# The place of n's own-column matmuls in the order of TensorE, in a convolution layer followed by a scan of GRU columns

## The chip, the cores and the metric

The kernel runs on one core of a Trainium2 chip. The metric is the device time of one execution in microseconds (us). A core has five engines that each work through their own queue: TensorE (PE, matmuls; its weight loads are shown apart as PEld), VectorE (DVE), ScalarE (ACT), GpSimd (POOL) and SyncE (SP, which issues transfers here). They meet through semaphores.

## The reference

The input x is 4 images of 64 channels by 256 by 256, in fp32. Layer 0 normalizes it by groups, runs a 1x1 and a depthwise 3x3 convolution, multiplies 8x8 patches in the frequency domain, normalizes and gates the product, projects it back and adds it to x. Layer 1 normalizes the sum by groups and then goes through it column by column. Each column depends on the one before it:

```python
def step(prev_col, cur_col):
    nb = jnp.concatenate([pad, prev_col, pad], axis=1)
    x = jnp.concatenate([nb[:, :-2], nb[:, 1:-1], nb[:, 2:]], axis=-1)
    new = _gru_cell(x.reshape(B * H, 3 * Cf), cur_col.reshape(B * H, Cf), ...)
# _gru_cell(x, h): i_r, i_z, i_n = x @ w_ih.T + b_ih;  h_r, h_z, h_n = h @ w_hh.T + b_hh
r = jax.nn.sigmoid(i_r + h_r)
z = jax.nn.sigmoid(i_z + h_z)
n = jnp.tanh(i_n + r * h_n)
return (1.0 - z) * n + z * h
```

So a row of the new column needs three neighbouring rows of the previous new column (the "taps") and one row of its own normalized input (the "own" part). The first column passes through unchanged; the other 255 are computed. The result is added to the layer's input.

## The kernel before, in words

Layer 0 works in 32 blocks and keeps TensorE busy with small fp32 matmuls. Its sums are written to a DRAM tensor `x1`. The change does not touch it.

Layer 1 starts with loads of the columns from `x1` (`load_columns`), eight columns to a buffer, and normalizes them eight columns ahead (`normalize`, on ScalarE, result `xn`). The two halves of the partitions hold the channels of different images, and `xt` is a copy of `xn` with the halves exchanged, brought by transfers on SyncE's queue, two columns at a time. The loop over `w` calls `column(w)` and then `add(w)`, in which GpSimd adds the new column to its input and, every second column, SyncE's queue stores two columns to the output.

`column(w)` lays down the matmuls. A column of 256 rows is cut in two ranges ("parts"). Part 0 of the next column is always one row shorter than the last, so that its taps need only rows of the previous column's part 0. The cut moves from 144 rows down to 113 in 32 columns, and then starts over at 144; then part 0 needs rows of both parts of the column before.

Every product with a weight is made as four matmuls on the four quarters of the array (`quarters`, 64 rows by 64 columns each), for two images a half. `own(ps, gate, h0, h1, stop)` issues the products with the column's own input: 8 matmuls in the executed program. `taps(ps, gate, h0, h1, start)` issues three neighbours: 24 matmuls. Gates go to four PSUM tiles of two banks each: `hn` (n's own part, for the whole column at once, never mixed with the taps since r multiplies it), `hr` (r: own and taps summed), `ni` (n's taps) and `hz` (z: own and taps). Each has one buffer, and the four fill the eight banks. `hr`, `ni` and `hz` are used by part 0 and then by part 1; `hn` is written once for a column and read by both parts. The trace calls them `pshn`, `pshr`, `psni` and `pshz`.

`state(w, part, ...)` turns these into the new rows. ScalarE makes g = sigmoid(hr), and then normalizes a column that will be needed eight columns later. VectorE multiplies g with `hn` (a scalar_tensor_tensor, `n<-pshn,bias_sb,g`), adds `ni`; ScalarE makes the tanh and z = sigmoid(hz); VectorE does `g<-xn,n`, `g<-g,z` and `st<-g,n`, and the last is the new state, which the next column's taps read.

All instructions of the kernel body pass through `InOrder`, which keeps each engine's queue in the order of the program's text. So what stands earlier in `column` comes earlier in TensorE's queue. A matmul that writes a PSUM tile must wait until its last readers are done: for `hn` that is the product of part 1 of the column before. Because of the recording layer, all lines of the trace read L156; tiles tell them apart.

Of the kernel before, what the change touches and what calls it, by code (L numbers as in the profile page):

```python
# [16 lines left out]
B, C, W, H = 4, 64, 256, 256  # L17
# [144 lines left out]
def tile_conv_then_gru(  # L162
# [521 lines left out]
    with ExitStack() as s:  # L684
# [60 lines left out]
        def parts(w):  # L745


            at = H // 2 + SKEW // 2 - (w - 1) % SKEW
            return (0, at), (at, H)
# [3 lines left out]
        def bank_pair(gate, w):  # L753
            return ps_g.tile([P, 2, 512], F32, tag=gate, name=f"ps{gate}_{w}")

        def quarters(ps, weights, rhs, start, stop):
            for r, c in QUARTERS:
                nc.tensor.matmul(
                    ps[c * C : (c + 1) * C, r],
                    lhsT=weights[r * C : (r + 1) * C],  # L760
                    rhs=rhs(r, c),
                    start=start,
                    stop=stop,
                    tile_position=(r * C, c * C),
                )

        def column(w):

            i, xn, xt, st = w % WB, xns[w // WB], xts[w // WB], stcols[(w - 1) // WB]

            def own(ps, gate, h0, h1, stop):

                quarters(
                    ps,
                    wh[:, gate, :],
                    lambda r, c: (xn[:, c] if r == c else xt)[r * C : (r + 1) * C, i, h0:h1],
                    True,
                    stop,
                )

            def taps(ps, gate, h0, h1, start):
                for t in range(3):
                    quarters(
                        ps,
                        wi[:, 3 * gate + t, :],
                        lambda r, c: st[r * C : (r + 1) * C, c, (w - 1) % WB, h0 + t : h1 + t],
                        start and t == 0,
                        t == 2,
                    )

            pn = bank_pair("hn", w)[:, :, 0:H]
            own(pn, 2, 0, H, True)
            for part in range(2):
                h0, h1 = parts(w)[part]
                pr, pi, pz = (bank_pair(gate, f"{w}_{part}")[:, :, 0 : h1 - h0] for gate in ("hr", "ni", "hz"))
                own(pr, 0, h0, h1, False)
                taps(pr, 0, h0, h1, False)
                taps(pi, 2, h0, h1, True)
                own(pz, 1, h0, h1, False)
                taps(pz, 1, h0, h1, False)  # L800
                state(w, part, pn[:, :, h0:h1], pr, pi, pz)

        def state(w, part, pn, pr, pi, pz):
            h0, h1 = parts(w)[part]
            i, num = w % WB, h1 - h0
            xn, st = xns[w // WB], stcols[w // WB]
            g = gk.tile([P, 2, MAX], F32, tag=f"g{part}", name=f"g_{w}_{part}")[:, :, 0:num]
            n = gk.tile([P, 2, MAX], F32, tag=f"n{part}", name=f"n_{w}_{part}")[:, :, 0:num]
            z = gk.tile([P, 2, MAX], F32, tag=f"z{part}", name=f"z_{w}_{part}")[:, :, 0:num]
            nc.scalar.activation(g, pr, AF.Sigmoid, bias=b_rz[:, 0:1], scale=1.0)  # L810
            if w + WB < W:
                normalize(w + WB, part)
            nc.vector.scalar_tensor_tensor(n, pn, bias_sb[:, 5:6], g, ALU.add, ALU.mult)
            nc.vector.tensor_tensor(n, pi, n, ALU.add)
            nc.scalar.activation(n, n, AF.Tanh, bias=bias_sb[:, 2:3], scale=1.0)
            nc.scalar.activation(z, pz, AF.Sigmoid, bias=b_rz[:, 1:2], scale=1.0)
            nc.vector.tensor_tensor(g, xn[:, :, i, h0:h1], n, ALU.subtract)
            nc.vector.tensor_tensor(g, g, z, ALU.mult)
            nc.vector.tensor_tensor(st[:, :, i, 1 + h0 : 1 + h1], g, n, ALU.add)
# [8 lines left out]
        for w in range(W):  # L828
            n, i = w // WB, w % WB
            if i == 0 and n + 1 < W // WB:  # L830
                empty_states(n + 1)
            if w:
                column(w)
            add(w)
            if i % 2 and w + 2 * WB < W:
                load_columns(w + 2 * WB - 1)
# [55 lines left out]
```

## Time and profile before

| what | value |
|---|---|
| median of 3 runs | 5957.78 us (5954.8 to 5962.69) |
| profiled execution: its own time | 5951.97 us |
| profiled execution: span, first to last instruction | 5950.2 us |
| mean granted TensorE clock | 0.994 |
| TensorE matmul busy | 5537.8 us (93%) |
| VectorE busy | 4085.5 us (69%) |
| ScalarE busy | 3465.8 us (58%) |
| GpSimd busy | 399.5 us (7%) |
| layer 1: first matmul of n to the end | 4383.2 to 5950.2 us |

The span is the time from the first to the last instruction of the profiled execution; its own time also holds what lies around these. Busy time of TensorE is modelled from pipelined matmuls, so a share of 93% doesn't say that no more matmuls would fit. A line of the order in time gives the start, the length, the engine, the operation, the tiles as out<-in with their shapes, how many instructions are merged, and in brackets the idle time of the engine before it and what ended this. A wait for several semaphores is put down to the one that came last.

### The profile page before, as it was taken

Reading aid. Unit: us, or ns where it says so; the run is one execution under the profiler, and the core shown is the slowest. Engines: PE = TensorE matmul, PEld = TensorE weight load, DVE = VectorE, ACT = ScalarE, POOL = GpSimd, SP = SyncE. Lnnn points to the kernel's source line nnn. Section 1 sums busy time; section 2 is a strip of 40 time slices with the busy share of each in tenths; the row PEclk is TensorE's granted clock in tenths of the full one; section 3 lists DMA queues with packets and bytes.
Section 4 is the critical chain, followed back from the end, with each engine's and each line's share of the span. In section 5 each row is a group of like instructions: output and inputs, shape, how many; then the busy total and the mean of one; then the engine's idle time right before and its main releaser. Section 6 shows DMA issues by size and latency. Waiting matters only on the chain.

```text
span 5950.2 us, 278865 instructions
## 1 busy us (share of the span) xinstructions
PE 5537.8 (93%) x127184; PEld 4770.7 (80%) x127184; DVE 4085.5 (69%) x9549; ACT 3465.8 (58%) x4617; POOL 399.5 (7%) x602
## 2 busy tenths in 40 slices
PE   5499999999999999999999999999979999999998
PEld 4478888888887888887888888888868888888887
DVE  7566776676676666676666767766666766676666
ACT  1256665666665656665565666565645555555555
POOL 0000000000000000000000000000002212122121
PEclk9999999999999999999999999999989999999999
DMA  9544545445445444444444554544444444444442
GB/s 384 213 133 144 139 132 147 121 141 144 140 126 142 137 135 141 140 134 133 143 124 138 146 144 123 149 131 132 128 119 113 113 113 113 113 112 113 111 113 80
DMA packets 549698, 817.79 MB, mean 137 GB/s; under 512 B 38443, under 2 KB 432436, under 8 KB 544404
## 3 DMA queue, kind: packets, MB, share of 16 engines
q1 hardware_dynamic: 523264, 683.80, 40.4%
q0 software_dynamic: 22320, 114.70, 5.8%
q8 instruction: 996, 16.32, 1.1%
q10 hardware_dynamic: 2934, 1.46, 0.1%
q14 instruction: 184, 1.51, 0.1%
HBM read 622.22 MB, written 144.05 MB: 129 GB/s over the span
## 4 chain that ended last, share of the span: by engine, by line
PE 64%; DVE 18%; ACT 7%; DMA 5%; issue 5%; SPq 0%; DVEq 0%; ACTq 0%; POOL 0%; POOLq 0%
PE psring L156 61%; DVE g L156 7%; DVE n L156 6%; DVE st L156 4%; ACT n L156 4%; DMA t<-t_all 2%; DMA xc<-in_x 2%; ACT v L156 2%; ACT z L156 1%; PE pshr L156 1%; PE pshz L156 1%; PE psni L156 1%; ACT h L156 1%; PE pshn L156 0%; SPq L156 0%
## 5 line engine op out<-in xcount | busy, mean ns | idle before, releaser
L156 PEld LDWEIGHTS psring<-h,t 100*32 100x32 f32 x40960 | 1336.1, 116 | 266.6 <-issue 184.8
L156 PE MATMUL psring<-h,t 100*32 100x128 f32 x40960 | 1437.4, 274 | 88.8 <-ACT h L156 35.6
L156 PEld LDWEIGHTS psring<-w_sb,xq 64*100 64x100 f32 x24576 | 1352.4, 163 | 86.1 <-issue 48.8
L156 PE MATMUL psring<-w_sb,xq 64*100 64x128 f32 x24576 | 1394.2, 271 | 27.3 <-POOL xq L156 17.8
L156 ACT COPY h<-psring 100x1024 f32<-100x1024 f32 x1274 | 1203.2, 1027 | 147.7 <-PE psring L156 140.9
L156 DVE TENSOR_TENSOR pr<-psring,q 128x512 f32<-128x512 f32 (+1 forms) x576 | 463.8, 860 | 338.6 <-PE psring L156 334.7
L156 DVE BATCH_NORM_STATS2 lnst<-z 128x6 f32<-128x64 f32 x4096 | 544.8, 212 | 118.7 <-ACT z L156 118.7
L156 DVE TENSOR_TENSOR z<-z,lnm 128x1024 f32<-128x1024 f32 x512 | 612.6, 1217 | 8.7
L156 ACT ACTIVATE n<-n,bias_sb 128x288 f32<-128x288 f32 (+7 forms) x510 | 259.8, 509 | 574.0 <-DVE n L156 574.0
L156 ACT COPY q<-psring 128x1024 f32<-128x1024 f32 x256 | 259.1, 1012 | 514.2 <-PE psring L156 457.6
L156 ACT COPY z<-psring 128x2048 f32<-128x2048 f32 x128 | 238.8, 1866 | 502.2 <-PE psring L156 485.1
L156 PE MATMUL psring<-pr,g_sb 32*64 32x512 f32 x8192 | 486.1, 598 | 7.2 <-issue 7.1
L156 ACT ACTIVATE y<-psring,ln_sb 128x512 f32<-128x512 f32 x512 | 372.1, 781 | 200.8 <-PE psring L156 197.2
L156 DVE COPY h<-psring 100x1024 f32<-100x1024 f32 x262 | 320.3, 1223 | 218.5 <-PE psring L156 216.2
L156 PE MATMUL pshr<-st,wi 64*64 64x144 f32 (+7 forms) x12240 | 433.3, 270 | 14.0 <-DVE st L156 13.4
L156 PE MATMUL psni<-st,wi 64*64 64x144 f32 (+7 forms) x12240 | 438.4, 270 | 8.0 <-issue 6.6
L156 DVE TENSOR_TENSOR g<-xn,n 128x288 f32<-128x288 f32 (+7 forms) x510 | 217.3, 426 | 325.2 <-ACT n L156 325.2
L156 PE MATMUL pshz<-st,wi 64*64 64x144 f32 (+7 forms) x12240 | 436.6, 269 | 1.8 <-issue 1.1
L156 DVE TENSOR_TENSOR y<-psring,y 128x1024 f32<-128x1024 f32 x256 | 312.3, 1220 | 122.7 <-ACT y L156 121.2
L156 POOL TENSOR_TENSOR raw<-raw,st 128x512 f32<-128x512 f32 x256 | 303.4, 1185 | 1208.1 <-DVE st L156 511.1
L156 PEld LDWEIGHTS pshr<-st,wi 64*64 64x64 f32 x12240 | 361.7, 133 | 17.0 <-issue 16.7
L156 PEld LDWEIGHTS psni<-st,wi 64*64 64x64 f32 x12240 | 361.5, 133 | 13.5 <-issue 9.9
(94 smaller groups left out, 6944.7 us busy)
## 6 DMA issues: line engine op xcount, KB each, us to landing
t<-t_all SPq DMA_DIRECT2D x768, 400.0 KB
xq<-in_xh POOLq DMA_DIRECT2D x128, 800.0 KB, 4.6
xc<-in_x SPq DMA_DIRECT2D x32, 2048.0 KB
xr<-in_x SPq DMA_DIRECT2D x256, 256.0 KB
x<-xr SPq DMA_DIRECT2D x256, 256.0 KB
raw<-x SPq DMA_DIRECT2D x128, 256.0 KB
raw<-x SPq DMA_DIRECT2D x256, 128.0 KB
xt<-xn SPq DMA_DIRECT2D x256, 128.0 KB
```

What stands on the lines that cost most here:

```text
L156: return self.tc.keep_in_program_order(got(*args, **kwargs))
```

## The change

In `column`, the call that issues n's own matmuls for the whole column moves from ahead of the loop over the two parts into it. In part 0 it now stands behind r's own matmuls and r's taps, and ahead of n's taps. Part 1 does not issue it, as before. The same matmuls are issued, with the same operands, into the same tiles.

```diff
             pn = bank_pair("hn", w)[:, :, 0:H]
-            own(pn, 2, 0, H, True)
             for part in range(2):
                 h0, h1 = parts(w)[part]
                 pr, pi, pz = (bank_pair(gate, f"{w}_{part}")[:, :, 0 : h1 - h0] for gate in ("hr", "ni", "hz"))
                 own(pr, 0, h0, h1, False)
                 taps(pr, 0, h0, h1, False)
+                if part == 0:
+                    own(pn, 2, 0, H, True)
                 taps(pi, 2, h0, h1, True)
                 own(pz, 1, h0, h1, False)
                 taps(pz, 1, h0, h1, False)
```

In the built program the order of VectorE, ScalarE, GpSimd and SyncE is the same as before. On TensorE each column's order becomes r of part 0, n's own part, n's taps of part 0, z of part 0, and then part 1 as before. VectorE's product of part 0 waits for TensorE and ScalarE, where it waited for ScalarE; r's taps of part 0 wait for VectorE by themselves.

## The prediction

> **What bounds the kernel now.** I read the share of each slice first, then the waits of layer 1, then the order in time of one column, then the chain of a column where the two ranges start over. The columns of layer 1 run from about 4,383 us to the end, 255 of them. In that stretch TensorE is busy 93% of the time (1394.5 of 1500 us from 4440 us on), VectorE 70%, ScalarE 58%. That looks like a TensorE bound, and the waits seem to agree (who waited | for whom: us in total, times, longest; 4650 to 5940 us):
>
> ```profile
> ACT n L156 <- DVE n L156: 482.2, 427, 2.1
> DVE g L156 <- ACT n L156: 273.0, 428, 1.0
> PEld pshn L156 <- DVE n L156: 115.1, 195, 0.9
> PE pshn L156 <- DVE n L156: 67.7, 179, 0.7
> PE pshr L156 <- DVE st L156: 11.5, 6, 1.9
> ```
>
> The third and fourth lines are what the change touches: TensorE waits for the one bank pair `hn`, which the product of part 1 of the last column (`n<-pshn`) still reads. But TensorE idles there, so it has time left; the first two lines are a loop between VectorE and ScalarE. VectorE over one column, in order of time (start, length, operation):
>
> ```profile
> 5200.53 0.40 DVE L156 TENSOR_TENSOR st<-g,n 128x230 f32<-128x230 f32 x1
> 5200.84 0.50 DVE L156 SCALAR_TENSOR_TENSOR n<-pshn,bias_sb,g 128x280 f32<-128x280 f32 x1
> 5201.45 0.45 DVE L156 TENSOR_TENSOR n<-psni,n 128x280 f32<-128x280 f32 x1
> 5202.55 0.45 DVE L156 TENSOR_TENSOR g<-xn,n 128x280 f32<-128x280 f32 x1 [0.66 <-ACT n L156]
> 5203.11 0.45 DVE L156 TENSOR_TENSOR g<-g,z 128x280 f32<-128x280 f32 x1
> 5203.60 0.45 DVE L156 TENSOR_TENSOR st<-g,n 128x280 f32<-128x280 f32 x1
> 5203.96 0.45 DVE L156 SCALAR_TENSOR_TENSOR n<-pshn,bias_sb,g 128x232 f32<-128x232 f32 x1
> ...
> 5206.47 0.40 DVE L156 TENSOR_TENSOR st<-g,n 128x232 f32<-128x232 f32 x1
> 5206.79 0.50 DVE L156 SCALAR_TENSOR_TENSOR n<-pshn,bias_sb,g 128x278 f32<-128x278 f32 x1
> ```
>
> Five instructions of part 0, five of part 1, the tanh the only idle time. The next column's product starts at 5206.79, 0.08 us before the last `st` ends (5206.47 + 0.40): back to back. From `st` to `st` it is 5.94 us. The same count over 248 columns gives a median of 5.96 us and 5.94 to 6.04 in nearly all. Does that product wait for TensorE? TensorE and ScalarE around it:
>
> ```profile
> 5204.47 0.43 PE L156 MATMUL pshn<-xn,wh 64*64 64x256 f32 x1 [0.49 <-DVE n L156]
> 5204.95 0.28 PE L156 MATMUL pshr<-xn,wh 64*64 64x139 f32 x1
> 5205.90 0.89 PE L156 MATMUL psni<-st,wi 64*64 64x139 f32 x24
> 5206.15 0.49 ACT L156 ACTIVATE g<-pshr,b_rz 128x278 f32<-128x278 f32 x1 [0.30 <-PE pshr L156]
> ```
>
> The sigmoid of r ends at 5206.64, and VectorE needs it at 5206.79. VectorE starts about 0.02 us after a ScalarE release (tanh 5201.99 + 0.53, next start 5202.55), so TensorE's order has 0.13 us to spare here. The VectorE-ScalarE loop sets the column. It isn't so in the columns where part 0 jumps from 113 to 144 rows (w = 33, 65, ... 225: seven, 7.8 us or more each) and in the first. Their chain:
>
> ```profile
> 4981.14 0.47 DVE st L156
> 4981.61 0.14 issue
> 4981.75 1.00 PE pshr L156 x24
> 4982.75 0.02 issue
> 4982.77 0.51 ACT g L156
> ```
>
> Here the taps of r need rows of part 1, so the path runs through TensorE.
>
> **What the Trainium skill says.** "PSUM — Partial Sum Buffer", section "Engine vs sequencer instructions": TensorE's matmuls start and complete in program order, so what stands behind the wait of n stands still too. The trace agrees: r's first matmul follows 0.48 us behind n's. "VectorE: DVE Perf Modes", section "Two Vector instructions with no wait between them": a wait handled by the sequencer alone doesn't make the next Vector instruction held behind the one before. The trace agrees, with numbers below. "TensorE: Matmul & The Clock Gate", section "What's actually happening": half clock until about 3.4 us of activity. In the first column r's matmuls follow each other at 0.24 us in one quarter, and a quarter later in the run takes 0.12.
>
> **The change part by part.** Nothing is added to or taken from the work: 8 matmuls with 8 weight loads (pshn) move behind 32 (pshr, part 0). No DMA moves. Times are against the profiled execution (span 5950.2, time 5951.97 us); the median of 5957.78 lies 5.8 us above that.
>
> *Ordinary columns, 246 or so.* r's own matmuls need only its bank (ScalarE freed it at 5203.24) and the column's input; its taps need `st` of part 0, at 5204.05. TensorE is done with z of part 1 at 5203.98. So r runs from about 5204.05, not 5204.95: 0.9 us earlier. n's matmuls (0.43 us when they follow other work) stand at about 5204.95 to 5205.4, and their bank is free since 5204.41: the wait of about 0.7 us is gone. Then n's input part, which needs its bank (5204.92), and z (its bank at 5205.84, wanted at about 5206.1). What is late next: nothing on VectorE. TensorE, early now, waits instead for the banks of part 1 and for `st` of part 0, about the same 0.6 us in all: from the start of one group to the next its seven take 0.48, 0.95, 0.71, 0.95, 0.79, 0.65 and 0.80 us, 5.33 in 5.95. VectorE still begins the product behind `st`. Gain: 0. The cover of r grows from 0.13 to some 0.4 us at ScalarE, over 1 us at TensorE.
>
> *Columns in which the cover failed.* In four the gap from `st` to the product is 0.05 to 0.17 us above its neighbours (near 4445, 5218, 5314, 5356), 0.46 us together. Gone with the larger cover: -0.5 us. Bounds 0 and -0.5.
>
> *First column.* TensorE is cold. The transfer of `xt` lands at 4398.72; n takes two matmuls a quarter at 0.48 us each before r's start at 4399.63. r would start 0.91 us earlier, and with it the table load, the sigmoid and the product (4404.08). n's input part ends where it did, at about 4402.9, still ahead of its add. -0.9 us; bounds 0 and -0.96.
>
> *The seven starts-over.* Before, n was done while TensorE waited for `st`. Now it stands between r and n's input part: r's taps start at 4981.75, the input part at 4982.51, its end is at 4983.45. With 0.43 us it ends at 4983.88, and its add started at 4983.93. n itself ends at about 4983.1, product at 4983.31. So the cover is just used up: 0 to 0.1 us each; I take 0.05, +0.4 us for seven. With no cover it would be at most 0.43 each, 3.0 us.
>
> *A second wait.* In the program as built, the product of part 0 waited for ScalarE alone; now it waits for TensorE and ScalarE, which puts a semaphore instruction ahead of it on VectorE. Behind it on VectorE stands the whole loop. Such an instruction is 0.021 us, and 0.044 us pass until the operation where it waits for the operation just before (add, `g<-g,z`). Where its semaphore had long come, the trace's records show no cost: 28 products of layer 0 (`pr<-psring,q` after another) begin 0.084 us before their forerunner's end with such an instruction, 290 without it begin 0.083 before; 64 `bn<-xr` with it 0.084 before. Here n is done more than 1 us ahead of need. I take 0. The far bound: overlap lost, as where `st` waits for `g<-g,z` (0.035 behind in place of 0.083 ahead), 0.118 us for each of 255, +30 us.
>
> *TensorE's own new wait.* r's taps now wait for `st` explicitly; about 0.14 us from `st` to the first tap (4981.61 to 4981.75), in front of more than 1 us of cover. 0.
>
> Sum: 0 - 0.5 - 0.9 + 0.4 + 0 = -1.0 us: 5951.0 profiled, 5956.8 as a median.
>
> **The rivals.** *The wait was on the path*: if the 0.71 us for `hn` came off each of some 250 columns, 178 us, 5780. For it: the largest wait of TensorE. Against it: VectorE shows no idle time but for the tanh. *The second wait costs* (slower): at the product of part 0, 0.118 us for 255, 5988; it decides from 0.05 us a column (12 us) on. For it: the longer gap of each two-wait instruction in the loop. Against it: those wait for their direct forerunner, this one doesn't. *Starts-over pay in full*: +3.0 in place of +0.4, 5959; no change that can be measured. *The reorder is not kept* by the recording layer: the program as built shows it in every column, so no chance.
>
> **How the numbers follow.** No change that can be told 0.93 (0.85 for my sum, 0.08 for starts-over or stalls of TensorE's issue falling elsewhere), the second wait 0.05, the wait on the path 0.02. About 0.2%, 12 us, is what a measurement here tells from no change. The three runs before spread over 7.9 us, from 3 below to 5 above their median; with the bounds of the small terms (-1.5 to +3) the range is 5951 to 5964. The far rivals, 0.07, stay outside.
>
> **What would show it.** TensorE's wait of `pshn` for VectorE near zero; new waits of `pshr` for `st` and of `psni`, `pshz` for part 0's banks, of like sum; the median column still 5.95 to 5.96 us; the sigmoid of r about 0.3 us earlier against the product. A column of 6.05 or more, with the product starting at `st`'s end or later, would make it wrong.

## The result and the profile after

| | before | after |
|---|---|---|
| median of 19 runs | 5961.25 us | 5968.89 us |
| ratio to before, 95% interval | | 1.0011, 1.0002 to 1.0019 |
| span of the profiled execution | 5950.2 us | 5967.8 us |
| first load of a column, start | 4378.43 us | 4389.09 us |
| 254 columns, from last `st` to last `st`, sum | 1533.75 us | 1542.04 us |
| of these the seven that start over | 57.23 us | 65.88 us |
| the other 247 | 1476.52 us | 1476.16 us |

From the third row on, the table shows the one profiled execution of each kernel. A column's time is counted from the start of the last `st` of the column before to the start of its own last `st`.

The kernel became slower. The ratio says 0.11%, or 6.6 us of 5961; the two medians differ by 7.6 us. This is under what I had called the bound of measurement and above what the interval leaves to chance. The spans of the profiled executions differ by 17.6 us, but 10.7 of it lie ahead of layer 1's first load, in code that is the same. The columns carry 8.3 us more, and all of it sits in seven of them.

In the ordinary columns the period stayed as forecast. VectorE in order of time, the kernel after:

```profile
5214.95 0.40 DVE L156 TENSOR_TENSOR st<-g,n 128x230 f32<-128x230 f32 x1
5215.26 0.50 DVE L156 SCALAR_TENSOR_TENSOR n<-pshn,bias_sb,g 128x280 f32<-128x280 f32 x1
5215.87 0.45 DVE L156 TENSOR_TENSOR n<-psni,n 128x280 f32<-128x280 f32 x1
...
5220.89 0.40 DVE L156 TENSOR_TENSOR st<-g,n 128x232 f32<-128x232 f32 x1
5221.21 0.50 DVE L156 SCALAR_TENSOR_TENSOR n<-pshn,bias_sb,g 128x278 f32<-128x278 f32 x1
```

From `st` to `st` it is again 5.94 us, and the product still begins 0.08 us before `st` ends, although a semaphore instruction now stands ahead of it. The trace's records give the median of this overlap for 254 products with that instruction, and for 509 without it in the kernel before: 0.084 us in both. The waits of TensorE, after (4650 to 5960 us):

```profile
PEld pshz L156 <- ACT z L156: 70.2, 252, 0.5
PEld psni L156 <- DVE n L156: 37.0, 163, 0.6
PE pshr L156 <- DVE st L156: 16.5, 7, 3.2
```

The 183 us of waits for `hn` are gone, and other waits stand in their place. The third line is the one to stop at: r's first taps wait for `st` for up to 3.2 us at a time, where the longest was 1.9 before. These are columns in which the ranges start over. The chain of one of them, w = 97, after:

```profile
4992.60 0.47 DVE st L156
4993.07 0.14 issue
4993.21 0.97 PE pshr L156 x24
4994.17 0.43 PE pshn L156 x8
4994.60 1.38 PE psni L156 x24
4995.98 1.94 PE pshz L156 x32
```

n's eight matmuls take their 0.43 us as expected. But n's taps take 1.38 us by the chain, and 1.29 from their start to z's (4994.40 to 4995.69), where the same 24 took 0.73 before, and z's 32 take 1.94. TensorE in order of time says why; first before, then after:

```profile
4978.92 0.43 PE L156 MATMUL pshn<-xn,wh 64*64 64x256 f32 x1 [0.31 <-DVE n L156]
...
4979.55 0.28 PE L156 MATMUL pshr<-xn,wh 64*64 64x144 f32 x1
4981.75 0.97 PE L156 MATMUL pshr<-st,wi 64*64 64x144 f32 x24 [1.92 <-DVE st L156]
4982.51 0.94 PE L156 MATMUL psni<-st,wi 64*64 64x144 f32 x24
4983.24 0.28 PE L156 MATMUL pshz<-xn,wh 64*64 64x144 f32 x1
```

```profile
4990.03 0.28 PE L156 MATMUL pshr<-xn,wh 64*64 64x144 f32 x1
4993.21 0.97 PE L156 MATMUL pshr<-st,wi 64*64 64x144 f32 x24 [2.89 <-DVE st L156]
...
4994.40 1.59 PE L156 MATMUL psni<-st,wi 64*64 64x144 f32 x24
4995.69 0.44 PE L156 MATMUL pshz<-xn,wh 64*64 64x144 f32 x1
```

Before, n's matmuls (4978.92 to 4979.4) and then r's own part stood in the middle of the wait for part 1's `st`; behind them TensorE idled 1.92 us. After, r's own part follows z at once, n must stay behind the taps, and the idle time is 2.89 us in one piece. A little later a matmul of 144 columns takes 0.44 us in place of 0.28. That is the clock, as the next view shows. Each of its lines is a stretch of 3.41 us, with the busy time of PE, PEld, DVE, ACT and POOL and the number of their instructions, then the granted clock of TensorE, the DMA engines' share and GB/s. After:

```profile
4991.13:4994.54 3.41, 1.33 (x37) 1.29 (x41) 1.37 (x3) 1.08 (x3) 1.09 (x1) 1.00 0.69 184
4994.54:4997.95 3.41, 3.41 (x68) 3.41 (x63) 1.43 (x3) 1.21 (x3) 0.00 (x0) 0.50 0.19 43
4997.95:5001.37 3.42, 3.42 (x132) 3.36 (x128) 2.06 (x5) 2.36 (x6) 0.00 (x0) 1.00 0.14 34
```

The clock is at half for exactly one such stretch (a "low stretch" from here on), just when n's taps and z run on the path, and 68 matmuls fall into it where the next has 132. In the trace after, each of the seven start-over columns has one low stretch. The kernel before had them in two of the seven (from 5368.61 and 5563.18 us), and I could have read them there. Before, a column without one and a column with one:

```profile
4979.49:4982.90 3.41, 1.49 (x49) 1.25 (x45) 1.37 (x3) 1.05 (x3) 1.10 (x1) 1.00 0.56 169
4982.90:4986.31 3.41, 3.41 (x140) 3.41 (x131) 2.10 (x5) 2.61 (x6) 0.00 (x0) 1.00 0.18 46
5365.20:5368.61 3.41, 1.27 (x28) 0.61 (x20) 2.44 (x6) 0.92 (x2) 0.17 (x2) 1.00 0.59 155
5368.61:5372.02 3.41, 3.33 (x56) 3.36 (x60) 0.63 (x2) 0.99 (x2) 1.09 (x1) 0.50 0.23 76
```

These stretches fall on a grid: within one trace all low stretches in the columns begin a whole multiple of 3.413 us apart (4605.42, 4799.98, 4994.54 us after: 57 of them each). So this grid of windows can be laid over the trace. In the two kernels, 876 windows lie between 4440 and 5935 us. The nine in which TensorE was busy for 0.39 of the window or less were followed by half clock; the others, from 0.438 up, were not. "TensorE: Matmul & The Clock Gate" of the Trainium skill, section "What's actually happening", has this window, its length of about 3.4 us and that it runs freely; it says the clock falls after an idle window. The runs differ from it in this: here a window that was busy for 39% (1.33 of 3.41 us) was enough.

The half clock also changes what n's new place costs. In w = 161 the low stretch starts within 0.1 us of r's first taps in both kernels (before 5368.61 and 5368.69 us, after 5383.66 and 5383.62 us). VectorE's product and add there, before, then after:

```profile
5371.01 0.52 DVE L156 SCALAR_TENSOR_TENSOR n<-pshn,bias_sb,g 128x288 f32<-128x288 f32 x1 [2.46 <-ACT g L156]
5371.91 0.46 DVE L156 TENSOR_TENSOR n<-psni,n 128x288 f32<-128x288 f32 x1 [0.39 <-PE psni L156]
```

```profile
5386.31 0.52 DVE L156 SCALAR_TENSOR_TENSOR n<-pshn,bias_sb,g 128x288 f32<-128x288 f32 x1 [2.84 <-PE pshn L156]
5387.48 0.46 DVE L156 TENSOR_TENSOR n<-psni,n 128x288 f32<-128x288 f32 x1 [0.65 <-PE psni L156]
```

Before, the product waits for r's sigmoid; after, it waits for n's matmuls, which take 0.86 us at half clock (5385.04 to 5385.90), and the add waits longer too. The column takes 8.88 us before and 9.49 after.

Was it so in other executions than the profiled ones? Each execution's mean granted clock is on record: 0.9929 on average over the 19 of the changed kernel, 0.9942 over 55 of the kernel before. A low stretch takes about 0.0003 off the mean (half of 3.41 us in some 5960). So I estimate four or five more low stretches per execution after the change; the two profiled ones have seven and two in the columns.

### The profile page after: what moved, and what is told of

Same layout as the page of the kernel before. It is cut to its first block, busy times and chain, and to the rows that moved or that the text cites. A ratio compares the mean times of both kernels' runs of the same rounds, so it can differ in the third digit from the quotient of the medians.

```text
span 5967.8 us, 279144 instructions
## 1 busy us (share of the span) xinstructions
PE 5600.8 (94%) x127184; PEld 4785.5 (80%) x127184; DVE 4085.0 (68%) x9549; ACT 3440.6 (58%) x4617; POOL 399.4 (7%) x602
## 4 chain that ended last, share of the span: by engine, by line
PE 65%; DVE 16%; ACT 7%; DMA 6%; issue 6%; SPq 0%; DVEq 0%; ACTq 0%; POOL 0%; POOLq 0%
PE psring L156 60%; DVE n L156 6%; DVE g L156 6%; ACT n L156 4%; DMA t<-t_all 3%; DVE st L156 3%; DMA xc<-in_x 2%; PE pshz L156 2%; ACT v L156 1%; PE pshr L156 1%; ACT z L156 1%; PE psni L156 1%; ACT h L156 1%; PE pshn L156 0%; SPq L156 0%
## 5 line engine op out<-in xcount | busy, mean ns | idle before, releaser
L156 PE MATMUL pshr<-st,wi 64*64 64x144 f32 (+7 forms) x12240 | 457.5, 273 | 23.1 <-DVE st L156 19.1
L156 PE MATMUL psni<-st,wi 64*64 64x144 f32 (+7 forms) x12240 | 460.8, 275 | 8.8 <-issue 6.0
L156 PEld LDWEIGHTS psni<-st,wi 64*64 64x64 f32 x12240 | 379.2, 134 | 78.4 <-DVE n L156 41.9
```

The lines of the kernel that those rows point to most:

```text
L156: return self.tc.keep_in_program_order(got(*args, **kwargs))
```

## The experiments

**The theory**: in the seven start-over columns the moved matmuls leave TensorE idle longer in one piece; a window falls to some 0.4 busy or less and the next one runs at half clock, on the path. **Rivals**: the second wait or the new order costs in all columns; n's 0.43 us cost where they now stand on the path; stalls in the issue of TensorE's instructions.

**Undo it in the seven columns.** Against the changed kernel:

```diff
+            over = w > 1 and (w - 1) % SKEW == 0
+            if over:
+                own(pn, 2, 0, H, True)
             for part in range(2):
...
-                if part == 0:
+                if part == 0 and not over:
                     own(pn, 2, 0, H, True)
```

> n stands ahead of r in the seven columns in which the ranges start over (w = 33, 65, ... 225), as before, and behind r in all others. Clock theory (TensorE idles longer in those seven, its clock is granted at half for 3.41 us, and the column runs on it): the seven go back from 9.27 to 9.69 us to 7.81, or 8.2 to 8.95 where a low stretch of the clock still falls on them as it did in two of them before; the other columns stay at 5.95; the 254 columns from state to state sum to about 1533 us (before 1533.75, after 1542.04); ratio to before 0.9997 to 1.0002. Rival, the second wait on VectorE or n's new place in the ordinary columns costs: the sum stays near 1542, ratio 1.0011.

Ratio 1.0000 (0.999 to 1.001); this and all ratios below are to the kernel before. The seven: six at 7.81 us and one at 8.94, with the one low stretch of the columns. Sum of the 254: 1534.15. The other 247 came to 1478.36. Over the seven runs with a cut over 32 columns these 247 lie between 1476.2 and 1479.6, with n ahead of r (three runs) as with n behind (four). So moving n in them costs nothing that these sums can show, and the loss is in the seven.

**Do it in the seven alone**: against the changed kernel, with the two conditions of the last run exchanged.

```diff
+            if not over:
+                own(pn, 2, 0, H, True)
...
-                if part == 0:
+                if part == 0 and over:
                     own(pn, 2, 0, H, True)
```

> The other half: n stands behind r only in the seven columns that start over. Clock theory: each of the seven takes 9.3 to 9.7 us with a stretch of 3.41 us at half clock in each; sum of the 254 columns 1542 to 1543 us; ratio 1.001 to 1.0015, as the whole change. Rival of the ordinary columns: sum about 1534, ratio 1.000.

Ratio 1.0018 (1.0010 to 1.0027), sum 1540.60: the loss is here. But only four of the seven took 9.24 to 9.49 us; the other three took 7.82, with n behind r as well, and had no low stretch. That missed the expectation, and it separates the two causes: the same order costs nothing where the clock stays. At w = 129 and w = 161 two windows split the idle time (busy 0.66 and 0.50, 0.50 and 0.68); at w = 225 it was short, 1.85 us, and its window busy for 0.46.

**Fill the idle time, leave n on the path.** The changed kernel, and n's matmuls issued three times more ahead of r in the seven columns. They write the same values that n writes later; this is extra work and leaves the result as it is.

```diff
             pn = bank_pair("hn", w)[:, :, 0:H]
+            over = w > 1 and (w - 1) % SKEW == 0
+            for _ in range(3 if over else 0):
+                own(pn, 2, 0, H, True)
```

> The change as it is, and in the seven columns n's eight matmuls are also issued three times ahead of r, with the same result in the same banks, so that TensorE idles less before r's taps; n still stands between r and its own taps on the path. Clock theory: no stretch at half clock in the columns, the seven take 7.8 to 7.9 us, sum about 1532, ratio 0.9993 to 1.0001. Rival, n's place on the path costs by itself (0.43 us of matmuls and what follows): the seven stay above 8.2 us at full clock; if all of the loss is place, at 9.3, and the ratio is 1.001.

There is no low stretch in the columns. Five of the seven take 7.81 to 7.82 us; in the other two (8.08 and 8.17) a single gap between VectorE's instructions is 0.25 or 0.35 us longer. In w = 129, with 8.08, TensorE's issue stalls for 0.21 us within r's taps of part 1, at full clock; what held the add back in w = 225 the trace doesn't show. Sum 1531.74, ratio 0.9991 (0.9981 to 1.0001), and the mean granted clock over 22 executions is 0.9950. The window over w = 97, and the matmuls in it:

```profile
4981.49:4984.90 3.41, 2.35 (x70) 2.00 (x64) 1.57 (x4) 1.08 (x3) 1.09 (x1) 1.00 0.46 137
```

```profile
4983.02 0.97 PE L156 MATMUL pshr<-st,wi 64*64 64x144 f32 x24 [1.06 <-DVE st L156]
...
4984.21 0.94 PE L156 MATMUL psni<-st,wi 64*64 64x144 f32 x24
4984.94 0.28 PE L156 MATMUL pshz<-xn,wh 64*64 64x144 f32 x1
```

With 24 more matmuls, but 2.35 of 3.41 us busy, n's taps are back at 0.73 us. At full clock n's place on the path costs 7.819 - 7.808 = 0.01 us a column: from the product's start to the add's it is 0.633 us where it was 0.622. So the place alone does not make the loss.

**The same filling in the kernel before**:

```diff
-            own(pn, 2, 0, H, True)
+            over = w > 1 and (w - 1) % SKEW == 0
+            for _ in range(4 if over else 1):
+                own(pn, 2, 0, H, True)
```

> The kernel before, with n's eight matmuls issued four times in place of once in the seven columns. Clock theory: the two of the seven that were slow before (8.88 and 8.95 us, each with a stretch at half clock) go to 7.81 as the rest, sum about 1531, and no stretch at half clock lies in the columns; ratio 0.9994 to 1.0000. Rival, these two were slow from stalls in the issue of TensorE's instructions: they or others stay at 8.2 to 9 us at full clock.

No low stretch in the columns; six of the seven at 7.80 to 7.81 us, one at 8.16 for a late add. The seven sum to 55.00 us in place of 57.23, so the two slow ones of before were the clock. The sum of all 254, 1533.60, did not fall, since the other 247 came to 1478.59, 2.1 us above before and within the spread given above; ratio 0.9997 (0.9985 to 1.0008), no change that can be told.

**Fill it a little.** The changed kernel with n's matmuls once more ahead of r:

```diff
+            over = w > 1 and (w - 1) % SKEW == 0
+            if over:
+                own(pn, 2, 0, H, True)
```

> The change, with n's eight matmuls issued once more ahead of r in the seven columns that start over: about 0.43 us of the idle time filled, where three rounds filled it enough. Reading of the runs so far: the clock goes to half for 3.41 us after a window of 3.41 us (on one fixed grid) in which TensorE is busy for 0.39 or less, and stays full from 0.44 on. So the windows at the seven should lie at about 0.44, as in the kernel before, where n's matmuls stood there: 0 to 2 of the seven slow (8.9 to 9.4 us), the rest 7.82. If the clock has nothing to do with the busy share, all seven stay above 9.2.

This run has one execution, the profiled one. Four of the seven were slow (9.39 to 9.74), three took 7.82 or 7.83. That is more than I had expected, but they sort by their windows: busy 0.33, 0.35, 0.42 and 0.44 were followed by half clock, 0.48, 0.50 and 0.58 were not. The window of w = 65 and the one after it:

```profile
4792.01:4795.42 3.41, 1.12 (x37) 0.90 (x32) 1.37 (x3) 0.86 (x2) 0.88 (x1) 1.00 0.52 155
4795.42:4798.83 3.41, 3.41 (x60) 3.21 (x56) 0.98 (x2) 1.45 (x3) 0.21 (x1) 0.50 0.21 53
```

Over the columns of all runs the border lies near 0.44 of this view's busy time: at 0.438 and 0.439 the clock stayed in the kernel before, and at 0.439 it fell here. But 0.44 is not a limit for all work. Layer 0 of the kernel before, with other matmuls, has a window that was busy for 0.53 and still was followed by half clock:

```profile
1542.28:1545.69 3.41, 1.80 (x65) 1.53 (x61) 2.41 (x3) 0.00 (x0) 0.00 (x0) 1.00 0.93 262
1545.69:1549.10 3.41, 3.41 (x67) 3.02 (x59) 0.00 (x0) 1.01 (x1) 0.00 (x0) 0.50 0.63 223
```

So it is not this busy time itself that decides; what is counted the trace doesn't show.

**A version built on this.** Since a start-over costs 1.85 us (7.81 - 5.96) even at full clock, the cut may move over more columns. Against the changed kernel: n behind r in ordinary columns, n ahead and four times where the ranges start over, and the cut over 64 columns:

```diff
-        SKEW = 32
+        SKEW = 64
...
+            over = w > 1 and (w - 1) % SKEW == 0
+            if over:
+                for _ in range(4):
+                    own(pn, 2, 0, H, True)
...
-                if part == 0:
+                if part == 0 and not over:
```

> A version built on this: n behind r in ordinary columns; n ahead, issued four times, where the ranges start over; and the cut moves over 64 columns in place of 32, so that it starts over in three columns (w = 65, 129, 193) and not in seven. Each start-over avoided is 7.81 - 5.96 = 1.85 us: sum of the 254 columns 1533.75 - 2.6 (no slow clock) - 7.4 = about 1524 us, ratio 0.998. Rival: with part 0 at up to 160 rows r's matmuls are no longer covered, columns above 5.96 us near the start of each cycle, sum not below 1530.

Sum 1524.80 us, median 5949.26, ratio 0.9979 (0.9970 to 0.9988): faster than the kernel before, and the sum as expected to a microsecond. The three start-overs take 7.98 us each.

**The cut over 128 columns**, otherwise the same:

```diff
-        SKEW = 64
+        SKEW = 128
```

> The same with the cut moving over 128 columns: one start-over (w = 129), part 0 from 192 down to 65 rows. If the cover holds: sum 1533.75 - 2.6 - 11.1 = about 1520 us, ratio 0.9972 to 0.998. Rival: r's and z's matmuls of the large part come late while the small part is short on VectorE, columns of 6.1 us or more over part of the cycle, and the sum comes out at or above that with 64 columns.

Sum 1522.81, 2 us less than with 64 and 3 us more than expected; ratio 0.9981 (0.9972 to 0.9990), not to be told from the one with 64. The ordinary columns hold 5.95 to 5.96 us with part 0 at 191 rows; in the last eight of a cycle the median is 5.98 to 6.00 (5.96 in these columns before), and the start-over takes 8.33.

**The cut over 128 columns with n ahead of r everywhere.** It asks whether the change's order is worth anything. Against the kernel before:

```diff
-        SKEW = 32
+        SKEW = 128
...
-            own(pn, 2, 0, H, True)
+            over = w > 1 and (w - 1) % SKEW == 0
+            for _ in range(4 if over else 1):
+                own(pn, 2, 0, H, True)
```

> The cut over 128 columns with n ahead of r everywhere, as before (four times where the ranges start over). Tells whether n behind r is worth something once the cover is needed: n's wait for its bank ends with part 1's product, and n 0.48, r 1.0 to 1.3 and the sigmoid 0.65 us follow one after the other while part 1 of 64 rows gives VectorE only about 2.2 us more of work. Theory: in columns with part 0 above about 160 rows the product waits, 0.1 to 0.4 us each, sum 5 to 12 us above the run with n behind r. Rival: the place of n makes no difference here either, sums equal within 1 us.

Ratio 1.0046 (1.0031 to 1.0060), sum 1560.37: 37.6 us above the same cut with n behind r, three times the upper end I had expected. Columns are at 6.72 us with part 0 near 190 rows and reach 5.95 only near 143. VectorE, ScalarE and TensorE there, w = 11, n ahead of r:

```profile
4489.70 0.31 DVE L156 TENSOR_TENSOR st<-g,n 128x146 f32<-128x146 f32 x1
4490.59 0.60 DVE L156 SCALAR_TENSOR_TENSOR n<-pshn,bias_sb,g 128x364 f32<-128x364 f32 x1 [0.58 <-ACT g L156]
```

```profile
4489.99 0.56 ACT L156 ACTIVATE g<-pshr,b_rz 128x364 f32<-128x364 f32 x1 [0.82 <-PE pshr L156]
```

```profile
4488.03 0.43 PE L156 MATMUL pshn<-xn,wh 64*64 64x256 f32 x1 [0.88 <-DVE n L156]
...
4488.82 1.10 PE L156 MATMUL pshr<-st,wi 64*64 64x182 f32 x24
```

The product waits for the sigmoid, and this for r; r stands behind n, and n waited 0.88 us for its bank, which the last column's product still read. In the run with n behind r, VectorE's waits over this stretch hold none for that sigmoid, and the same two instructions at this size lie back to back:

```profile
4470.88 0.31 DVE L156 TENSOR_TENSOR st<-g,n 128x148 f32<-128x148 f32 x1
4471.11 0.60 DVE L156 SCALAR_TENSOR_TENSOR n<-pshn,bias_sb,g 128x362 f32<-128x362 f32 x1
```

## Why the prediction was wrong

The median came to 5968.9 us, above the range of 5951 to 5964. Of the 12.1 us above the forecast, 3.5 are a median of before that moved from 5957.8 (3 runs) to 5961.3 (19 runs), 1.0 is the gain that I had forecast, and 7.6 is the change. (The range is also narrower than its own terms: 5957.8 with 3 below, 5 above and -1.5 to +3 for the small terms gives 5953 to 5966. That would not have held the result either.)

*What bounds it*: right. The VectorE-ScalarE loop sets an ordinary column at 5.95 us, and 183 us of TensorE's waits were worth nothing.

*Ordinary columns, 0*: right (1476.52 to 1476.16 us, with a spread of some 3 us over the runs). The cover grew by the 0.3 us that I had said, from a higher start: from the end of r's sigmoid to the product the median of part 0 went from 0.33 to 0.63 us, where the one column I had read has 0.15.

*The second wait, 0*: right; the overlap is 0.084 us with and without it.

*First column, -0.9*: right in sign. From the first load to the first product it was 25.65 before and 24.33 after. This time also holds transfers and varies: with n ahead of r in the first column it was 24.76 to 26.10 in four runs (25.63 in the mean), with n behind r 24.33 to 25.23 in six (24.86), a difference of 0.8 us.

*Columns in which the cover failed, -0.5*: the four named ones lost their excess (0.17, 0.15, 0.09 and 0.06 us). Single gaps of 0.35 us that came and went in other columns are larger, so the sum doesn't show it.

*The seven start-overs, 0 to 0.1 us each, "at most 0.43"*: this step failed. I costed only what n's matmuls add behind r, and put at nothing what their leaving takes from the time ahead of r. There they had kept TensorE busy inside a wait. Without them the idle time came to 2.2 to 3.2 us, one window of the clock fell to 0.23 to 0.39 busy, and the next ran at half clock: 8.65 us more for the seven together, +1.24 each in the mean. The upper bound of 3.0 us, and with it the range, left this out. The place itself costs 0.01 us at full clock, less than I took. At half clock it costs some 0.5 us: start-overs with a low stretch take 8.92 us in the mean where n stands ahead of r (three columns of two runs) and 9.41 in the mean of the seven after. So I estimate, from these means, that some 5.5 of the 8.65 us come from five more low stretches at 1.1 us and some 3.4 from n's place in all seven, less 0.35 for one late add before. I had named the clock for the first column alone, and had put the two slow start-overs of before, 8.88 and 8.95 us, down to nothing in particular, though a low stretch falls on each of them too.

*TensorE's own new wait, 0*: right in itself; from the end of `st` to r's first tap it is 0.14 us in w = 97 as it was. The longer idle time ahead of it belongs to the step that failed.

## What to carry to other kernels

Work that an engine does inside a wait is not free to move, even if the wait hides it: on TensorE it also keeps the clock up for what comes right after the wait. Before a matmul is moved out of an idle stretch (1.92 us here), lay windows of 3.41 us over it and ask how busy they stay; 24 spare matmuls ahead of the wait cost no time here and kept full clock, 8 did not in four of seven columns. An order that brings only slack is worth nothing until something uses the slack: with the cut over 128 columns the same order was worth 37.6 us.

## What the runs showed of the hardware

In the columns, TensorE's granted clock fell to 0.50 for one window of 3.41 us after a window that was merely under some 0.44 busy; in layer 0 a window busy for 0.53 had the same result. The windows lie on a grid fixed within each execution, so that one and the same order took 7.82 us in one column and 9.39 in another, as they happened to fall. In the changed kernel the low stretches lie 194.56 us apart, 57 windows of 3.413 us, so each start-over met the grid at a similar place: r's first taps lie between 1.3 us ahead of the low stretch's start and 0.4 us behind it. That this is why all seven were slow is a reading; no run varied the distance between start-overs alone.
